# Regrouping the matmuls of an attention kernel's prelude by kind, and a second buffer for the staged value products

## The chip, the core and the metric

The kernel runs on one core of one Trainium2 chip, all in fp32. The metric is device time in microseconds of one execution; the time shown is the median of several executions. Lower is better.

## What is computed

One gated cross-attention block with a feed-forward layer behind it, for x of shape (4, 2048, 512) and a context of shape (4, 77, 384), with 16 heads of 64:

```
n   = layernorm(x)
sim = (n @ Wq)_h @ (ctx @ Wk)_h^T * 64**-0.5          # per head h, 77 keys
att = softmax(sim) @ (ctx @ Wv)_h                     # heads joined again
x   = x + tanh(g_xattn) * (att @ Wo + bo)
x   = x + tanh(g_ffn) * (layernorm(x) @ W[k] + b[k])  # k = argmax(log_softmax(logits) + gumbel(u)), of 8
```

## The kernel before

The kernel folds weights together once, in a prelude, and then works on 16 groups of 512 tokens. For every head it needs two products that don't depend on the tokens. M is the head's query weight, with its row means taken out, times the head's keys (512 features by 80 padded keys by 4 batches). VO is the head's values times its slice of Wo (320 padded key rows by 512 features). With these a group needs three large products: scores = x M, attention output = p VO, feed-forward = y W. Each is done by `Seven`, a Strassen-Winograd scheme: seven products of half-size blocks instead of eight, with sums of the operand blocks made beforehand. For the operands that stay, `weight_sum(w, n)` makes them: blocks 0 to 3 of `m` hold M, `weight_sum(m, 0)` fills block 5, `(m, 1)` changes block 3, `(m, 2)` fills block 4 and `(m, 3)` fills block 6. For the moving ones, `xc[i].sum("T1")` to `sum("T4")` make them in `tq`. `product(s)` issues the matmuls of step s and `post(s)` takes a finished partial sum out of PSUM into `snap`, or adds it there. Steps 0, 2, 4 and 6 of a `Seven` go on adding to the same PSUM bank, so step 2 must wait until `post(0)` has copied what step 0 left.

The order on every engine is written by hand: the statements run in program order, and each engine keeps that order. Seven PSUM banks are handed out in turn. The SP queue issues nearly all DMAs, in order.

The prelude before the change, with the lines of the profile:

- `project_k(p)` (L266, evicted by ScalarE at L271) and `centre_wq(p)` (L283 to L291) for the eight pairs p of heads.
- `build_m(q, ...)` makes two of the four 128-feature quarters of M. One `m_head` is one matmul with 64 rows of contraction (L296), and two copies out of PSUM (L302 into `m` for batch 0, L303 into a staging area for batches 1 to 3). Quarters with even number are copied by ScalarE, odd ones by VectorE. The two heads of a pair lie in the two halves of the array's rows and are issued alternately.
- `project_v(p)` makes the values of one pair: three matmuls with 128 rows (L266) and one copy (L276) by ScalarE and VectorE in turn. Before the change each of the eight calls stands behind one pair's four `m_head` in `build_m`.
- The staging areas of M are `stages[0]` (blocks 4 to 6 of `m`), `stages[1]` and `stages[2]` (the two halves of `vo`) and `stages[3]` (`m_st`, in the buffer that later holds the scores `s`). At the end of each half of M four DMAs (L315, 960 KB each) store two areas to DRAM.
- `build_vo(p, engines)` makes VO of one pair: six matmuls with 64 rows (L331, the last two with 64 columns), six copies with a scale (L334 on VectorE, L336 on ScalarE), and four DMAs to DRAM (L340, 512 KB, and L341, 128 KB). The staging for the copies is `vo_st`, five areas in `vo`.
- `gates0` to `gates2` compute the two tanh and the choice k in small VectorE and ScalarE instructions; `gather()` (L246, L248) fetches row block k of W and of b by indirect DMA from the GpSimd queue. `sum_wf` (L631 to L633, GpSimd) and `mean_wf` (L639, a matmul with a tile of ones, and the copy L640) take the column means of W.
- Then come group 0's scores in three `Seven`: s0 for two of the five chunk pairs, s1 for two, s2 for one. Before the change pair 0 of VO stands ahead of s0, and pairs 1 and 2 stand behind steps 2 and 5 of s0. `x_columns` (L407) and `s_rows` (L515) are 32 by 32 transposes on VectorE. Pairs 3 to 7 of VO are made between group 1's scores, before and after the change.

Of the kernel before, what the change touches and what calls it, by code (L numbers as in the profile page):

```python
# [14 lines left out]
P = 128  # L15
# [4 lines left out]
def flamingo_block_kernel(  # L20
# [33 lines left out]
    nc = tc.nc  # L54
    NT, D = x.shape
# [7 lines left out]
    NP = H // 2  # L63
# [4 lines left out]
    KH = NK // 2  # L68
# [5 lines left out]
    T2 = T // 2  # L74
    NG = T // 32
# [12 lines left out]
    def bank(name):  # L88
        return pm.tile([P, 512], F32, tag="mm", name=name)

    m_d = dp.tile([B - 1, P, 4, 2, KH * P], F32, name="m_d")
    vo_d = dp.tile([H, BP, D], F32, name="vo_d")
# [3 lines left out]
    BLK = {(0, 0): 0, (0, 1): 1, (1, 1): 2, (1, 0): 3}  # L96
    m = cp.tile([P, 7, 2, KH, P], F32, tag="m")
# [7 lines left out]
    snap = cp.tile([P, NCC * ID], F32, tag="snap")  # L105
# [8 lines left out]
    def flat(t):  # L114
        n = len(t.shape) - 1
        names = " ".join("abcdef"[:n])
        return t.rearrange(f"p {names} -> p ({names})")

    def weight_sum(w, n, engine=None):

        to, a, b_, op = ((5, 0, 3, ALU.subtract), (3, 3, 2, ALU.add), (4, 3, 0, ALU.subtract),
                         (6, 1, 4, ALU.subtract))[n]
        (engine or nc.gpsimd).tensor_tensor(flat(w[:, to]), flat(w[:, a]), flat(w[:, b_]), op)

    m_f, vo_f, wf_f = flat(m), flat(vo), flat(wf)
# [6 lines left out]
    def row_tile(name):  # L132
        return wp.tile([P, NG, P], F32, tag="row", name=name, bufs=3)
# [9 lines left out]
    t = wp.tile([P, NK * T + KH * T2], F32, tag="pT", name="wq")  # L143
# [3 lines left out]
    xg, ys, ts_ = {}, {}, {}  # L147
# [41 lines left out]
    def by_chunk(t):  # L189

        return t.rearrange("p (a q e) -> p q a e", a=NA, e=32)

    def chunked(t):
        return t.rearrange("p (q a e) -> p q a e", a=NA, e=32)
# [21 lines left out]
    def gates0():  # L216
        nc.scalar.activation(tg, gg, AF.Tanh)
        nc.vector.tensor_reduce(st[:, 0:1], lg, AX.X, ALU.max)
        nc.vector.tensor_scalar(z, lg, st[:, 0:1], None, ALU.subtract)
        nc.scalar.activation(ez, z, AF.Exp)  # L220

    def gates1():
        nc.vector.tensor_reduce(st[:, 1:2], ez, AX.X, ALU.add)
        nc.scalar.activation(st[:, 2:3], st[:, 1:2], AF.Ln)
        nc.scalar.activation(l2, uu, AF.Ln)
        nc.scalar.activation(l2, l2, AF.Ln, scale=-1.0)

    def gates2():
        nc.vector.tensor_scalar(z, z, st[:, 2:3], None, ALU.subtract)
        nc.vector.tensor_tensor(z, z, l2, ALU.subtract)  # L230
        nc.vector.tensor_reduce(st[:, 3:4], z, AX.X, ALU.max)

        nc.vector.tensor_scalar(ez, z, st[:, 3:4], None, ALU.is_equal)
        nc.vector.tensor_tensor(ez, ez, rev, ALU.mult)
        nc.vector.tensor_reduce(st[:, 4:5], ez, AX.X, ALU.max)
        nc.vector.tensor_scalar(st[:, 5:6], st[:, 4:5], -1.0, float(OPS), ALU.mult, ALU.add)
        nc.vector.tensor_scalar(st[:, 6:7], st[:, 5:6], float(D), None, ALU.mult)
        nc.vector.tensor_scalar(st[:, 7:8], st[:, 5:6], float(NA), None, ALU.mult)
        nc.vector.tensor_scalar(rows[:, :NDC], rows[:, :NDC], st[:, 6:7], None, ALU.add)
        nc.vector.tensor_scalar(rows[:, NDC:], rows[:, NDC:], st[:, 7:8], None, ALU.add)  # L240
        nc.vector.tensor_copy(rows_u, rows)
    def gather():
        t = row_tile("wfr").rearrange("p g j -> p (g j)").rearrange("p (c d) -> p c d", c=NDC)
        for c in range(NDC):
            at = bass.IndirectOffsetOnAxis(ap=rows_u[:, c : c + 1], axis=0)
            nc.gpsimd.indirect_dma_start(out=t[:, c, :], out_offset=None, in_=W, in_offset=at)  # L246
        at = bass.IndirectOffsetOnAxis(ap=rows_u[:, NDC:], axis=0)
        nc.gpsimd.indirect_dma_start(out=bf_r, out_offset=None,  # L248
                                     in_=b.rearrange("o (a j) -> (o a) j", j=P), in_offset=at)
        nc.gpsimd.tensor_scalar(bo_c, bo_c, tgx, None, ALU.mult)  # L250
        nc.gpsimd.tensor_scalar(bf_r, bf_r, tgf, None, ALU.mult)
        return t
# [20 lines left out]
    def project_v(p):  # L273
        d = vT[p].rearrange("p r b k -> p b k r")
        copy = nc.vector.tensor_copy if p % 2 else nc.scalar.copy
        copy(d, project(wv, p, cT).rearrange("p (b k r) -> p b k r", b=B, r=R))  # L276
# [25 lines left out]
        copy(to_m[:, :, q % 2, :, ts(h, R)], src[:, 0].rearrange("p (o k) r -> p o k r", o=2))  # L302
        copy(to_d, src[:, 1:])  # L303

    def build_m(q, p0, p1, stages, v0=None):

        for p in range(p0, p1):
            for dq, dh in ((0, 0), (1, 1), (1, 0), (0, 1)):
                m_head(q + dq, 2 * p + dh, stages[dq])
            if v0 is not None:  # L310
                project_v(v0 + p - p0)
        if p1 == NP:
            for dq in range(2):
                for o in range(2):
                    nc.sync.dma_start(  # L315
                        out=m_d[:, :, BLK[o, (q + dq) // 2], (q + dq) % 2].rearrange("b p k -> p b k"),
                        in_=stages[dq][:, :, ts(o, KH * P)])


    vo_st = []  # L320

    def build_vo(p, engines):
        n = 0
        for c in range(3):
            r = min(P, BP - c * P)
            for hh in range(2):
                stg = vo_st[(2 * p + hh) % len(vo_st)]
                hr = ts(hh, DH)
                v = vT[p][hr].rearrange("p r b k -> p (r b k)")
                ps = bank("ps_vo")  # L330
                nc.tensor.matmul(ps[:r, :], v[:, ds(c * P, r)], wo[hr, p, :], start=True, stop=True)  # L331
                src, dst = by_chunk(ps[:r, :]), chunked(stg[:r, c, :])
                if engines[n % len(engines)] == "D":
                    nc.vector.tensor_scalar(dst, src, tgx[:r], None, ALU.mult)  # L334
                else:
                    nc.scalar.activation(dst, src, AF.Copy, scale=tgx[:r])  # L336
                n += 1
        for hh in range(2):
            d, stg = vo_d[2 * p + hh], vo_st[(2 * p + hh) % len(vo_st)]
            nc.sync.dma_start(out=d[0 : 2 * P].rearrange("(c r) e -> r c e", r=P), in_=stg[:, 0:2])  # L340
            nc.sync.dma_start(out=d[2 * P :], in_=stg[: BP - 2 * P, 2])  # L341

# [151 lines left out]
    norms, xc, yc, sc, pT = ({} for _ in range(5))  # L494

    def x_columns(i):
        t = column_tile("xc")
        tqs = {f"T{n + 1}": tq[:, n] for n in range(4)}
        xc[i] = Columns(t, **tqs)
        for q in range(NDC):  # L500
            to_columns(t, xg[i], q)
# [90 lines left out]
    def store(f, g0=0, n=NG, queues=(nc.sync,)):  # L592
        for a in range(NA):
# [4 lines left out]
    stages = [t[:, : (B - 1) * NK * P].rearrange("p (b k) -> p b k", b=B - 1) for t in  # L598
              (m_f[:, 4 * 2 * KH * P :], vo_f, vo_f[:, NP * D :], s_f)]
# [9 lines left out]
    for a in range(NA):  # L609
        nc.gpsimd.dma_start(out=bo_c[ts(a, 32)], in_=bo[ts(a, P)].rearrange("(q e) -> e q", e=32))  # L610
    nc.sync.dma_start(out=wo, in_=Wo.rearrange("(c p) f -> p c f", p=P))
    build_m(0, 0, NP // 2, stages[:2])
    build_m(0, NP // 2, NP, stages[:2], 0)
    x_columns(0)
    for t in ("T1", "T2", "T3", "T4"):
        xc[0].sum(t)
    weight_sum(m, 0)
    build_m(2, 0, 2, stages[2:], NP // 2)
    gates0()
    build_m(2, 2, NP // 2, stages[2:], NP // 2 + 2)  # L620
    gates1()
    build_m(2, NP // 2, NP, stages[2:])
    for n in range(1, 4):
        weight_sum(m, n, nc.gpsimd if n == 3 else nc.vector)
    for u_ in (vo_f[:, : NP * D], vo_f[:, NP * D :]):
        for e in range(u_.shape[1] // (3 * D)):
            vo_st.append(u_[:, ts(e, 3 * D)].rearrange("p (c e) -> p c e", c=3))

    def sum_wf(wfr):
        t = wf_f[:, :D]  # L630
        nc.gpsimd.tensor_tensor(t, wfr[:, 0, :], wfr[:, 1, :], ALU.add)  # L631
        nc.gpsimd.tensor_tensor(t, t, wfr[:, 2, :], ALU.add)
        nc.gpsimd.tensor_tensor(t, t, wfr[:, 3, :], ALU.add)  # L633

    wf_mean = wf_f[:, ds(5 * D, D)]

# [29 lines left out]

    n = norms[0]
    norms[1] = n1 = Norms(1)
    build_vo(0, "AD")
    s0 = scores0(0)  # L670
    for s in range(6):
        s0.product(s)
        if s == 0:
            gates2()
            wfr = gather()
        if s in (2, 5):
            build_vo(1 + s // 3, "AD")
        if s == 3:
            n.stats(xg[0], 0, 0, NG)
        s0.post(s)  # L680
    x_columns(1)
    for k in range(2):
# [106 lines left out]
    for i in range(1, NGRP):  # L789
        j, f, nx = i - 1, i - 2, i + 1  # L790
        n = norms[i]
# [126 lines left out]
        for s in range(6):  # L918
# [16 lines left out]
            if 2 <= s:  # L935
                k = (0, 2, 3, 5, 6)
# [6 lines left out]
    n = norms[NGRP] = Norms(NGRP)  # L943
# [145 lines left out]
```

## Time and profile before

| | before |
|---|---|
| median of 3 runs | 1253.28 us (1252.87 to 1254.22) |
| the profiled execution's own time | 1252.23 us |
| its span, first to last instruction | 1250.3 us |
| TensorE matmul busy | 1237.8 us, 99% |
| VectorE, ScalarE, GpSimd busy | 911.6, 683.0, 888.9 us |
| granted TensorE clock | 0.997 |

The profile is of one execution. Its page gives the busy time of each engine, the span in 40 slices, the DMA queues, the chain of waits that ended last, and groups of instructions by source line. "PE" is TensorE, "DVE" VectorE, "ACT" ScalarE, "POOL" GpSimd. A matmul of fp32 stands as two instructions in the trace. Two matmuls in different row halves of the array overlap, so their durations may not be added up; the distance from one start to the next may.

### The profile page before, as it was taken

What the parts mean: (1) busy time and instruction counts of PE and PEld (TensorE: products, weight loads), DVE (VectorE), ACT (ScalarE), POOL (GpSimd) and SP (SyncE); (2) the same over time, 40 slices, a digit from 0 to 9 for tenths busy, and PEclk for the clock granted to TensorE, in tenths of its full rate; (3) what the DMA queues carried; (4) which work ended last, traced back from release to release, by engine and by line L of the source; (5) the groups of instructions that cost most, each with busy time, mean ns of one, the idle gap of its engine ahead of it and who ended that gap; (6) DMA issues with size and microseconds to landing.
All of it is one profiled execution on the core that took longest, in us unless ns stands there. A gap on an engine that the chain in (4) does not pass through costs nothing.

```text
span 1250.3 us, 16985 instructions
## 1 busy us (share of the span) xinstructions
PE 1237.8 (99%) x5704; PEld 1059.4 (85%) x5704; DVE 911.6 (73%) x1855; ACT 683.0 (55%) x1957; POOL 888.9 (71%) x482
## 2 busy tenths in 40 slices
PE   9999999999999999999999999999999999999996
PEld 6575888888888888888888888888888888888885
DVE  5789876667976766787776767776776877766577
ACT  3539554738274573827456382745638274564823
POOL 4348885867967786685968778575977877575766
PEclk9999999999999999999999999999999999999998
DMA  9777300314014030303106030212305120010102
GB/s 261 296 210 237 92 1 1 68 42 110 1 34 118 1 68 1 68 23 106 26 1 152 1 68 2 48 20 85 68 1 112 41 57 12 1 34 1 34 2 67
DMA packets 95221, 80.27 MB, mean 64 GB/s; under 512 B 3856, under 2 KB 83088, under 8 KB 95136
## 3 DMA queue, kind: packets, MB, share of 16 engines
q1 hardware_dynamic: 92768, 76.74, 24.1%
q10 hardware_dynamic: 1760, 1.34, 0.4%
q0 software_dynamic: 608, 1.13, 0.3%
q8 instruction: 45, 0.74, 0.3%
q14 instruction: 40, 0.33, 0.1%
HBM read 44.07 MB, written 35.13 MB: 63 GB/s over the span
## 4 chain that ended last, share of the span: by engine, by line
PE 94%; DVE 3%; ACT 1%; POOL 1%; issue 0%; DVEq 0%; ACTq 0%; POOLq 0%
PE ps_s L461 37%; PE ps_a L461 36%; PE ps_f L461 15%; PE ps_kv L266 2%; PE ps_vo L331 2%; PE ps_m L296 2%; ACT s L532 1%; POOL s L543 1%; DVE s L515 1%; DVE pT L552 0%; PE ps_w L167 0%; DVE snap L486 0%; DVE t L412 0%; DVE vo L334 0%; DVE sm L539 0%
## 5 line engine op out<-in xcount | busy, mean ns | idle before, releaser
L461 PE MATMUL ps_a<-pT,vo 128*128 128x256 f32 x2240 | 486.2, 379 | 0.0
L461 PEld LDWEIGHTS ps_a<-pT,vo 128*128 128x128 f32 x2240 | 425.6, 190 | 57.9
L532 ACT ACTIVATE s<-s,nmx,up 128x77 f32<-128x77 f32 x1024 | 355.6, 446 | 0.8 <-DVE nmx L526 0.8
L432 POOL TENSOR_TENSOR pT<-pT 128x1280 f32<-128x1280 f32 x64 | 185.8, 2904 | 171.9 <-PE ps_a L461 162.3
L461 PE MATMUL ps_s<-tq,m 128*128 128x256 f32 x1280 | 290.8, 380 | 0.3 <-ACT snap L467 0.3
L461 PEld LDWEIGHTS ps_s<-tq,m 128*128 128x128 f32 x1280 | 242.5, 190 | 36.7 <-issue 1.6
L467 ACT COPY snap<-ps_s 128x512 f32<-128x512 f32 (+1 forms) x188 | 93.5, 514 | 287.6 <-DVE t L412 131.4
L461 PE MATMUL ps_s<-xc,m 128*128 128x256 f32 x960 | 221.4, 380 | 0.0
L461 PEld LDWEIGHTS ps_s<-xc,m 128*128 128x128 f32 x960 | 182.0, 190 | 29.0 <-DVE vo L334 2.4
L543 POOL TENSOR_TENSOR s<-s,sm 128x1232 f32<-128x1232 f32 x64 | 145.2, 2270 | 48.2 <-DVE sm L540 48.1
L486 DVE TENSOR_TENSOR snap<-snap,ps_s 128x512 f32<-128x512 f32 (+1 forms) x141 | 83.5, 593 | 122.0 <-PE ps_s L461 117.9
L461 PE MATMUL ps_f<-tq,wf 128*128 128x256 f32 x512 | 118.5, 379 | 0.5 <-DVE snap L486 0.4
L552 DVE STREAM_TRANSPOSE pT<-s 128x512 f32<-128x512 f32 x160 | 101.0, 677 | 16.8 <-POOL s L543 16.8
L432 POOL TENSOR_TENSOR tq<-xc,tq 128x512 f32<-128x512 f32 x64 | 85.3, 1332 | 34.8 <-PE ps_f L461 32.3
L393 POOL TENSOR_TENSOR r<-r,neghalf 32x16 f32<-32x16 f32 (+1 forms) x33 | 93.1, 2831 | 23.1 <-DVE r L388 22.6
L461 PEld LDWEIGHTS ps_f<-tq,wf 128*128 128x128 f32 x512 | 97.1, 190 | 14.4 <-issue 0.7
L539 DVE TENSOR_REDUCE sm<-s 128x16 f32<-128x1232 f32 x64 | 91.5, 1429 | 20.7 <-ACT s L532 20.6
L515 DVE STREAM_TRANSPOSE s<-snap 128x512 f32<-128x512 f32 x156 | 99.8, 684 | 6.1 <-ACT snap L467 3.9
L524 DVE TENSOR_REDUCE ps_st<-s 128x16 f32<-128x1232 f32 x64 | 92.4, 1444 | 2.1
L432 POOL TENSOR_TENSOR tq<-xc 128x512 f32<-128x512 f32 x64 | 81.5, 1273 | 13.6 <-DVE xc L407 12.3
L461 PE MATMUL ps_f<-xc,wf 128*128 128x256 f32 x384 | 90.7, 379 | 0.0
L467 ACT COPY snap<-ps_f 128x512 f32<-128x512 f32 x63 | 36.9, 585 | 88.9 <-PE ps_f L461 85.9
(127 smaller groups left out, 1186.0 us busy)
## 6 DMA issues: line engine op xcount, KB each, us to landing
xg<-in_x_dram SPq DMA_DIRECT2D x64, 256.0 KB, 5.6
out_dram<-y SPq DMA_DIRECT2D x60, 256.0 KB, 4.2
vo<-vo_d SPq DMA_DIRECT2D x16, 640.0 KB, 5.6
vo_d<-vo SPq DMA_DIRECT2D x16, 512.0 KB, 3.5
m<-m_d SPq DMA_DIRECT2D x12, 640.0 KB, 4.0
m_d<-vo SPq DMA_DIRECT2D x4, 960.0 KB, 6.1
wq<-in_WqT_dram SPq DMA_DIRECT2D x8, 256.0 KB, 7.0
wq<-in_Wo_dram SPq DMA_DIRECT2D x1, 2048.0 KB
```

The lines of the kernel that those rows point to most:

```text
L266: nc.tensor.matmul(ps[:, :n], w[:, c, ts(p, P)], keys[:, c].rearrange("p b j -> p (b j)"), start=(c == 0), stop=(c == NCC - 1))
L393: nc.gpsimd.tensor_tensor(r, r, neghalf[:32, : r.shape[1]], ALU.pow)
L432: (engine or nc.gpsimd).tensor_tensor(self.at[name], self.at[a], self.at[b_], op)
L461: nc.tensor.matmul(self.ps[r][:, n, :], self.w(blk, c, pair), self.cols(cname, c), start=(first and n == 0 and c == 0), stop=(c == h - 1), ...
L467: nc.scalar.copy(dst, self.ps[r])
L486: nc.vector.tensor_tensor(c, c, self.ps[r], ALU.add)
L515: nc.vector.transpose(key_chunk(sc[i], k), cols.rearrange("p (g h r) -> p g h r", h=HA, r=R))
L524: nc.vector.tensor_reduce(mx, head(i, h), AX.X, ALU.max)
L532: nc.scalar.activation(head(i, h)[:, g, :], head(i, h)[:, g, :], AF.Exp, scale=norms[i].up[:, g : g + 1], bias=nmx[h][:, g : g + 1])
L539: nc.vector.tensor_reduce(sm, head(i, h), AX.X, ALU.add)
L543: nc.gpsimd.tensor_tensor(head(i, h), head(i, h), sums[h].unsqueeze(2).to_broadcast([P, NG, J]), ALU.mult)
L552: nc.vector.transpose(pT[i].all[:, k, :].rearrange("p (g h r) -> p g h r", h=HA, r=R), key_chunk(sc[i], k))
```

## The change

M is built in two runs of 32 heads with nothing between the heads, and the values of all eight pairs are made between the two runs. The smaller work of the prelude (x_columns of group 0 and its sums, the gates, the statistics of group 0) stands between the values now. Three pairs of VO follow the second run in a row, and then group 0's scores with no VO inside s0. Pair 0 of VO is staged in `snap`, which is free of the value weights by then; later pairs use the five areas in `vo`. Quarter 3 of M is stored behind pair 0's VO. `weight_sum(m, 1)` and `(m, 2)` move from VectorE to GpSimd, and `gather()` stands behind the weight sums.

```diff
-    def build_m(q, p0, p1, stages, v0=None):
-        for p in range(p0, p1):
+    def build_m(q, stages):
+        for p in range(NP):
             for dq, dh in ((0, 0), (1, 1), (1, 0), (0, 1)):
                 m_head(q + dq, 2 * p + dh, stages[dq])
-            if v0 is not None:
-                project_v(v0 + p - p0)
-        if p1 == NP:
-            for dq in range(2):
-                for o in range(2):
-                    nc.sync.dma_start(
-                        out=m_d[:, :, BLK[o, (q + dq) // 2], (q + dq) % 2].rearrange("b p k -> p b k"),
-                        in_=stages[dq][:, :, ts(o, KH * P)])
+    def store_m(q, stage):
+        for o in range(2):
+            nc.sync.dma_start(out=m_d[:, :, BLK[o, q // 2], q % 2].rearrange("b p k -> p b k"),
+                              in_=stage[:, :, ts(o, KH * P)])
+    def stage_of(h):
+        return vo_st[h if h < 2 else 2 + (h - 2) % (len(vo_st) - 2)]
...
-    build_m(0, 0, NP // 2, stages[:2])
-    build_m(0, NP // 2, NP, stages[:2], 0)
-    x_columns(0)
-    for t in ("T1", "T2", "T3", "T4"):
-        xc[0].sum(t)
-    weight_sum(m, 0)
-    build_m(2, 0, 2, stages[2:], NP // 2)
-    gates0()
-    build_m(2, 2, NP // 2, stages[2:], NP // 2 + 2)
-    gates1()
-    build_m(2, NP // 2, NP, stages[2:])
-    for n in range(1, 4):
-        weight_sum(m, n, nc.gpsimd if n == 3 else nc.vector)
-    for u_ in (vo_f[:, : NP * D], vo_f[:, NP * D :]):
+    for u_ in (snap, vo_f[:, : NP * D], vo_f[:, NP * D :]):
...
+    build_m(0, stages[:2])
+    for q in range(2):
+        store_m(q, stages[q])
+    for p in range(NP):
+        project_v(p)
+        if p == 0:
+            x_columns(0)
+            for t in ("T1", "T2", "T3", "T4"):
+                xc[0].sum(t)
+            weight_sum(m, 0)
+        if p == 2:
+            gates0()
+        if p == 3:
+            gates1()
+        if p == 4:
+            norms[0].stats(xg[0], 0, 0, NG)
+        if p == 6:
+            gates2()
+    build_m(2, stages[2:])
+    store_m(2, stages[2])
+    for n in range(1, 4):
+        weight_sum(m, n)
+    wfr = gather()
+    build_vo(0, "AD")
+    store_m(3, stages[3])
+    for p in range(1, 3):
+        build_vo(p, "AD")
...
-    build_vo(0, "AD")
     s0 = scores0(0)
     for s in range(6):
         s0.product(s)
-        if s == 0:
-            gates2()
-            wfr = gather()
-        if s in (2, 5):
-            build_vo(1 + s // 3, "AD")
-        if s == 3:
-            n.stats(xg[0], 0, 0, NG)
         s0.post(s)
```

More of the change, by code (lines that the diff above doesn't have):

```diff
@@ L326, in build_vo @@
             for hh in range(2):
-                stg = vo_st[(2 * p + hh) % len(vo_st)]
+                stg = stage_of(2 * p + hh)
                 hr = ts(hh, DH)
@@ L338, in build_vo @@
         for hh in range(2):
-            d, stg = vo_d[2 * p + hh], vo_st[(2 * p + hh) % len(vo_st)]
+            d, stg = vo_d[2 * p + hh], stage_of(2 * p + hh)
             nc.sync.dma_start(out=d[0 : 2 * P].rearrange("(c r) e -> r c e", r=P), in_=stg[:, 0:2])
```

## The prediction

> **What bounds the kernel now.** I read the page first (busy times and the chain of waits), then the chain in order of time for the first 80 us, then the timelines of VectorE, GpSimd and the SP queue beside it.
>
> ```profile
> PE 1237.8 (99%) x5704; PEld 1059.4 (85%) x5704; DVE 911.6 (73%) x1855; ACT 683.0 (55%) x1957; POOL 888.9 (71%) x482
> PE 94%; DVE 3%; ACT 1%; POOL 1%; issue 0%; DVEq 0%; ACTq 0%; POOLq 0%
> ```
>
> TensorE is the bound, end to end. Its only waits after the start are 0.35 us ahead of one score matmul and 0.4 us in the last part. So whatever TensorE saves in the prelude comes off the end, if nothing else becomes late. The chain in order of time (start, length, what) shows how long each kind of matmul takes in each neighbourhood:
>
> ```profile
> 5.98 12.44 PE ps_kv L266 x48
> 18.42 5.60 PE ps_m L296 x40
> 24.02 1.81 PE ps_kv L266 x6
> 25.84 1.28 PE ps_m L296 x8
> ...
> 47.47 4.51 PE ps_m L296 x32
> 51.97 2.72 PE ps_vo L331 x12
> 54.70 5.38 PE ps_s L461 x24
> 60.07 2.95 PE ps_vo L331 x12
> 63.02 5.38 PE ps_s L461 x24
> 68.40 2.97 PE ps_vo L331 x12
> 71.37 0.03 issue
> 71.40 0.07 DVE vo L334
> ...
> 72.73 2.40 DVE xc L407 x4
> 75.13 1.20 DVE s L515 x2
> ...
> 76.41 0.59 ACT snap L467
> 77.05 5.45 PE ps_s L461 x24
> ```
>
> The reader is to compare like with like. Eight M instructions take 1.12 us inside a run (5.60 / 5) and 1.28 us between values. Six value instructions take 1.81 us; by the key run (12.44 / 48, times 320 / 308 columns) they should take 1.62. A VO pair takes 2.72 us behind M, which also uses 64 rows, and 2.95 behind scores.
>
> **The change part by part.** Time zero for each part is T, the end of the last M matmul (51.97 before).
>
> *M and values.* One value group between M groups costs (1.81 - 1.62) + (1.28 - 1.12) = 0.35 us, so 0.18 per change between 64-row and 128-row matmuls. After the change: 128 M instructions at 0.1405 = 17.98, 48 value instructions at 0.2693 = 12.93, two changes 0.35; 31.26 instead of the 33.55 from 18.42 to 51.97. Saved 2.3 us; T becomes 49.7.
>
> *VO and scores.* Before, from T to the restart at 77.05, 25.08 us. After: three VO pairs at 2.72 = 8.16, nine score steps of eight matmul instructions at 0.216 (9.50 us for 44 later on) = 15.54, one change 0.2; 23.9. Saved 1.2 us, of which 0.35 is the stall. That stall is s1's `post(0)` behind VectorE's last VO copy, x_columns and s_rows. Without the VO copy (0.74) the row of VectorE work is 0.67 + 2.4 + 1.2, ScalarE adds 0.6, and TensorE has three steps, 5.2 us, to do meanwhile; nothing is left over, nothing is gained beyond. A VO pair behind a VO pair isn't in the trace: between 2.56 (no change of mode) and 2.95, and I take 2.72, the row that follows another 64-row kind; that is -0.3 to +0.5 us for two pairs.
>
> *Copies out of PSUM.* The M runs are longer now, with VectorE and ScalarE taking every other head:
>
> ```profile
> 19.41 0.23 DVE L302 COPY m<-ps_m 128x80 f32<-128x80 f32 x1
> 19.56 0.40 DVE L303 COPY vo<-ps_m 128x240 f32<-128x240 f32 x1
> 19.87 0.23 DVE L302 COPY m<-ps_m 128x80 f32<-128x80 f32 x1
> ```
>
> From head to head VectorE needs 0.46 us when it is behind (19.41 to 19.87), ScalarE 0.36 to 0.39, and TensorE delivers one per engine each 0.56. The Trainium skill speaks against the change here: "TensorEngine Tiling (Array Packing)", Performance Considerations, says that tiling speeds up TensorE but not the copies out of PSUM, which can become the bound. With the durations as they stand (0.24 + 0.40 = 0.64 a head) that would be so: 16 heads take 10.2 us against 9.0, and with the lag that VectorE brings to the second run the seven banks (1.7 us of matmuls ahead) would be short by about 0.9 us. The starts decide, since neighbouring copies overlap: 0 us, up to 0.9 in the range.
>
> *What moves onto VectorE between the values:* x_columns 2.5, gates0 and gates1 0.6, the statistics 3.2, gates2 2.2, four value copies of 0.78. From 28.0 (end of M's copies) and held to the values' own times this ends at 41.9, TensorE starts the second run at 40.6. The lag of 1.3 us fits into the banks (head 6 needs the last value's bank at 42.3). If gates2's first instruction is held up as before (1.17 us beside GpSimd's weight sum, against 0.2 for its like), M waits 0.6 us. x_columns needs group 0's tokens: their four loads were issued by 18.0 and take 9 us, before 28.
>
> *Weight sums on GpSimd.* Three of 2.9 us from T + 0.6 to T + 9.4. Step 1 of s0 uses the first at T + 10.1, step 2 the second at T + 11.8, step 5 the third at T + 17; hidden. VectorE loses 3.0 us of work, which nobody was waiting for.
>
> *DMAs and the SP queue.* M's first four stores are issued at 28 rather than 33.9, but wait in the queue behind Wo, whose bytes are followed by M's without a gap before the change too; they still end near 46, and the sum into block 5 still starts near 42.5. After T the order is two M stores, four of pair 0, two M stores, then pairs 1 and 2. New waits: s0's `post(0)` (ScalarE, with all later posts behind it, and TensorE's step 2 waiting) needs the first store of pair 0 out of `snap`. M's stores began to move at 53.5 and ran 960 KB in 2.5 us, the first landing 0.6 us after its last byte. So two M stores end at T + 6.5, 512 KB more at T + 7.9, landed at T + 8.5; `post(0)` wants it at T + 10.1. Hidden with 1.6 us left for ScalarE, 2.5 in all before a matmul is late. [...]The later posts need pair 0's other stores, 0.8 MB more, at T + 11.8: 2 us of bytes, so T + 10.5, hidden too. Pair 2 goes where quarter 2 of M was staged; landing T + 7.1, wanted T + 6.3 to 7.2; its banks are wanted at T + 10. The last M store holds the buffer of the scores: its bytes end near T + 16, s_rows wants it at T + 22.
>
> *The gather* is issued at T + 9.4 as before (61.44), now behind weight sums instead of behind gates2. TensorE reaches the ones-matmul at T + 29.1 instead of 30.4 (82.33).
>
> ```profile
> 75.47 0.60 POOL L251 TENSOR_SCALAR bf_r<-bf_r,tg 128x128 f32<-128x128 f32 x1 [7.57 <-DMA bf_r<-in_b_dram,rows_u]
> 78.73 1.27 POOL L633 TENSOR_TENSOR wf<-wf,wfr 128x512 f32<-128x512 f32 x1
> ```
>
> GpSimd waited for the gather until T + 23.5 and had the sum at T + 28.0. So 1.1 us of slack is left of 2.3: zero cost if the gather lands as before, and all that it is later by beyond 1.1 otherwise.
>
> Sum: 2.3 + 1.2 = 3.5 us off the profiled 1252.23, that is 1248.7 (span 1246.8). The median of the runs stands 1.05 us above the profiled execution: 1249.8.
>
> **The rivals.**
>
> *Gather a little late.* The DMA queue holds 4.6 MB of stores when the gather starts, against some 2.5 before. For it: the four row fetches already took 9.9 us each. Against it: with stores pending before, they moved 1 MB in about 6 us beside them. Two to three us later costs 1 to 2: 1250.8 to 1251.8, within 0.2% of before. Chance 0.14.
>
> *Smaller savings*: VectorE's lag reaches the banks (0.6 to 0.9), or VO pairs in a row cost 2.95 each (0.5): 1250.4 to 1251.2. Chance 0.12.
>
> *The gather comes last (slower).* If its packets move only after the stores and group 2's token loads, which follow in the same queue: 5.9 MB from T + 6.5 at 390 KB/us, and the loads, in 512-byte pieces, at half of that, end near T + 27; then the gather 2.7, GpSimd 4.6: the sum at T + 35, TensorE idle for 5.9 us at the ones-matmul: 1255.7. It decides from where b's row lands after T + 28.1 (before: T + 23.5). Against it: the fair share seen before. Chance 0.10; another 0.04 for a wait on pair 0's store of the same size.
>
> *Nothing changes* because TensorE isn't freed: the excess of 0.18 per change stands in every neighbourhood, so I give that no share of its own.
>
> **How the numbers follow.** The likeliest case, 0.60, is 3.5 us saved, 1248.8 to 1250.6. A measurement of this kernel can tell about 0.2% (2.5 us) from no change, so faster means below 1250.8. With the edge of the second rival: faster 0.62, within 0.2% 0.24, slower 0.14. The range reaches from the likeliest case with cheap VO pairs (1248.8) over the two mild rivals to the runs' own spread: 1252.8.
>
> **What would show it.** Right: the chain has one M run of 9.0 us from 18.4, values of 13 us, M again, T at 49.7; VO 8.1 us; scores undivided to a step at T + 23.9 with no idle time; ScalarE's first copy into `snap` waiting for TensorE, not for a DMA. Wrong: idle TensorE at the ones-matmul behind GpSimd; M instructions above 0.15 us in the second run behind VectorE; "snap" waiting on the VO store.

## The result, and the profile after

| | before | after |
|---|---|---|
| median of 7 runs each | 1253.50 us (1252.36 to 1254.22) | 1249.18 us (1248.72 to 1249.89) |
| the profiled execution: span, own time | 1250.3, 1252.23 us | 1247.1, 1249.17 us |

The ratio is 0.9967, with a 95% interval of 0.9958 to 0.9977: the changed kernel is faster by 0.33%. Line numbers after are those of before plus one from `build_vo` on (VO L332, scores L462, VectorE's posts L487), and the ones-matmul is L655.

First the page of the changed kernel (busy times, and the shares of the chain of waits), then its chain in order of time: start, length, what.

```profile
PE 1234.9 (99%) x5704; PEld 1061.0 (85%) x5704; DVE 908.8 (73%) x1853; ACT 683.6 (55%) x1957; POOL 894.8 (72%) x484
PE 94%; DVE 2%; ACT 1%; DMA 1%; POOL 0%; issue 0%; SPq 0%; DVEq 0%; ACTq 0%; POOLq 0%
```

```profile
6.45 12.44 PE ps_kv L266 x48
18.89 8.81 PE ps_m L296 x64
27.71 13.12 PE ps_kv L266 x48
40.83 8.81 PE ps_m L296 x64
49.64 8.57 PE ps_vo L332 x36
58.21 21.04 PE ps_s L462 x96
79.25 0.86 PE ps_w L655 x2
```

TensorE runs the prelude in five unbroken pieces (keys, M, values, M, VO), then the scores. The same number of matmuls takes 2.9 us less busy time than before (1234.9 instead of 1237.8). From 18.89 to 49.64 M and the values take 30.75 us instead of 33.55. Its waits, over the whole span (what waited, for what, total us, times, longest):

```profile
PE ps_w L167 <- DVE tq L163: 1.5, 1, 1.5
PE ps_f L462 <- DVE snap L487: 0.4, 1, 0.4
```

The stall of 0.35 us ahead of s1 is gone, and no new one has come. The timelines of ScalarE (first line) and GpSimd show why; the bracket is the idle time before an instruction and what ended it:

```profile
60.21 0.58 ACT L468 COPY snap<-ps_s 128x512 f32<-128x512 f32 x1 [1.29 <-PE ps_s L462]
50.08 8.83 POOL L123 TENSOR_TENSOR m<-m 128x1280 f32<-128x1280 f32 x3 [5.47 <-ACT m L302]
72.74 0.60 POOL L251 TENSOR_SCALAR bf_r<-bf_r,tg 128x128 f32<-128x128 f32 x1 [7.20 <-DMA bf_r<-in_b_dram,rows_u]
76.00 1.27 POOL L621 TENSOR_TENSOR wf<-wf,wfr 128x512 f32<-128x512 f32 x1
```

`post(0)` waited for TensorE, not for the store of pair 0. The three weight sums end at 58.9. GpSimd had the gathered row of b at 72.7 and the sum of W's rows at 77.3; TensorE came for it at 79.3, so about 2.0 us were to spare.

**A ruler for all runs.** The profiles show that the prelude's first matmul of M starts anywhere from 18.1 to 19.4 us, with the warm-up ahead of it, whatever the kernel. So spans are compared in three stretches between starts of TensorE instructions: A from the first M matmul to the first of VO, B from there to the ones-matmul, C from there to the first feed-forward matmul with an operand out of `tq`. After that point every kernel of the study takes 1079.4 to 1079.8 us more. Each row of A, B and C is one profiled execution (us).

| kernel | A | B | C | A+B+C | median of its runs | ratio to before, 95% |
|---|---|---|---|---|---|---|
| before | 33.46 | 30.52 | 88.56 | 152.54 | 1253.9 beside the experiments | |
| after | 30.65 | 29.62 | 88.56 | 148.83 | 1249.18 | 0.9967 [0.9958, 0.9977] |
| after_again | 30.65 | 29.62 | 88.55 | 148.82 | 1249.69 | 0.9962 [0.9949, 0.9976] |
| m_only | 30.80 | 35.39 | 88.68 | 154.87 | 1254.38 | 1.0005 [0.9996, 1.0013] |
| m_alone | 30.65 | 33.74 | 88.56 | 152.95 | 1254.21 | 1.0002 [0.9993, 1.0011] |
| m_old_staging | 30.65 | 30.52 | 88.57 | 149.74 | 1249.76 | 0.9967 [0.9955, 0.9979] |
| values_in_twos | 33.60 | 29.62 | 88.57 | 151.79 | 1251.38 | 0.9981 [0.9974, 0.9988] |
| vo_only | 34.47 | 33.69 | 88.68 | 156.84 | 1256.59 | 1.0024 [1.0017, 1.0030] |
| vo_alone | 34.46 | 31.49 | 89.29 | 155.24 | 1255.82 | 1.0020 [1.0011, 1.0030] |
| vo_gather_first | 38.32 | 31.51 | 88.57 | 158.40 | 1258.55 | 1.0037 [1.0023, 1.0051] |
| m_stores_first | 30.65 | 33.33 | 88.56 | 152.54 | 1252.83 | 0.9995 [0.9986, 1.0004] |
| gather_late | 30.65 | 33.26 | 89.29 | 153.20 | 1252.91 | 0.9998 [0.9989, 1.0007] |
| vo_full_width | 30.65 | 28.77 | 89.27 | 148.69 | 1249.28 | 0.9965 [0.9951, 0.9978] |
| three_full_width | 30.65 | 28.77 | 88.58 | 148.00 | 1248.45 | 0.9955 [0.9942, 0.9969] |

The change saves 2.81 in A and 0.90 in B, and keeps all of it in C.

### The profile page after: what moved, and what is told of

It is laid out like the page before. It is cut to its first block, busy times and chain, and to the rows that moved or that the text cites. A ratio compares the mean times of both kernels' runs of the same rounds, so it can differ in the third digit from the quotient of the medians.

```text
span 1247.1 us, 16992 instructions
## 1 busy us (share of the span) xinstructions
PE 1234.9 (99%) x5704; PEld 1061.0 (85%) x5704; DVE 908.8 (73%) x1853; ACT 683.6 (55%) x1957; POOL 894.8 (72%) x484
## 4 chain that ended last, share of the span: by engine, by line
PE 94%; DVE 2%; ACT 1%; DMA 1%; POOL 0%; issue 0%; SPq 0%; DVEq 0%; ACTq 0%; POOLq 0%
PE ps_s L462 37%; PE ps_a L462 36%; PE ps_f L462 15%; PE ps_kv L266 2%; PE ps_vo L332 2%; PE ps_m L296 1%; ACT s L533 1%; DVE s L516 0%; DMA vo<-vo_d 0%; DVE pT L553 0%; PE ps_w L167 0%; DVE t L413 0%; DMA vo_d<-vo 0%; DVE snap L487 0%; POOL xc L559 0%
## 5 line engine op out<-in xcount | busy, mean ns | idle before, releaser
L462 PE MATMUL ps_a<-pT,vo 128*128 128x256 f32 x2240 | 486.2, 379 | 0.0
L462 PEld LDWEIGHTS ps_a<-pT,vo 128*128 128x128 f32 x2240 | 425.6, 190 | 57.9
L462 PE MATMUL ps_s<-tq,m 128*128 128x256 f32 x1280 | 290.6, 380 | 0.0
L462 PEld LDWEIGHTS ps_s<-tq,m 128*128 128x128 f32 x1280 | 242.6, 190 | 36.2 <-issue 1.6
L462 PE MATMUL ps_s<-xc,m 128*128 128x256 f32 x960 | 221.0, 379 | 0.0
L462 PEld LDWEIGHTS ps_s<-xc,m 128*128 128x128 f32 x960 | 182.2, 190 | 27.5 <-DVE vo L335 1.6
L487 DVE TENSOR_TENSOR snap<-snap,ps_s 128x512 f32<-128x512 f32 (+1 forms) x141 | 83.7, 593 | 130.4 <-PE ps_s L462 126.3
L462 PE MATMUL ps_f<-tq,wf 128*128 128x256 f32 x512 | 118.5, 379 | 0.5 <-DVE snap L487 0.4
L462 PEld LDWEIGHTS ps_f<-tq,wf 128*128 128x128 f32 x512 | 97.1, 190 | 14.4 <-issue 0.7
L462 PE MATMUL ps_f<-xc,wf 128*128 128x256 f32 x384 | 90.7, 379 | 0.0
```

The costliest lines, as they stand in the source:

```text
L462: nc.tensor.matmul(self.ps[r][:, n, :], self.w(blk, c, pair), self.cols(cname, c), start=(first and n == 0 and c == 0), stop=(c == h - 1), ...
L487: nc.vector.tensor_tensor(c, c, self.ps[r], ALU.add)
```

## The experiments

**M's two runs by themselves: m_only, m_alone, m_old_staging.** m_only is the changed kernel with pairs 1 and 2 of VO back inside s0:

```diff
-    for p in range(1, 3):
-        build_vo(p, "AD")
...
         s0.product(s)
+        if s in (2, 5):
+            build_vo(1 + s // 3, "AD")
```

> The changed kernel with pairs 1 and 2 of VO put back behind steps 2 and 5 of group 0's first score product; the two M runs and the values between them stay. Theory (each change of TensorE between 64-row and 128-row matmuls costs about 0.18 us): the stretch from the first M matmul to the last takes 30.7 us as in the changed kernel instead of 33.55, so about 2.8 us of the gain stay and 0.9 to 1.3 us are lost: 1250.0 to 1250.8. Rival (the gain comes from group 0's scores, where the stall of 0.35 us and VectorE's late copies were): most of the gain is lost, 1252 or more.

A fell to 30.80 as the theory has it, and the whole gain was lost again in B, which is 35.39 instead of the changed kernel's 29.62. The trace gave the wait to GpSimd's weight sums:

```profile
PE ps_s L462 <- POOL m L123: 3.0, 1, 3.0
```

So the first theory was that the sums are hidden only behind three VO pairs. m_alone tests it by putting two of the sums back on VectorE:

```diff
     for n in range(1, 4):
-        weight_sum(m, n)
+        weight_sum(m, n, nc.gpsimd if n == 3 else nc.vector)
```

> The kernel before with the M part alone (M in two runs with all values between them, its norms, gates and stores as in the change), VO pairs where they were, and the sums of slices 1 and 2 on VectorE as before, so that the first scores do not wait for GpSimd as in m_only. Theory (the two parts add, and m_only lost its gain only by that wait): M and values take 30.8 us instead of 33.55, no wait of TensorE for GpSimd ahead of step 1 of s0, the stall of 0.35 us ahead of s1 stays; median about 2.6 us under the kernel before (ratio 0.998). Rival (VectorE's two sums of 1.49 us, standing between the last M copies and pair 0's copies, now come when TensorE is 2.8 us earlier and hold it): 1 to 2 us of the gain lost, ratio 0.9988 to 0.9993.

That theory fell: the wait was again 3.0 us long. The trace of m_alone shows the real releaser (timelines of GpSimd, ScalarE and TensorE, one line each):

```profile
53.81 2.89 POOL L123 TENSOR_TENSOR m<-m 128x1280 f32<-128x1280 f32 x1 [8.96 <-DVE m L123]
58.85 0.58 ACT L468 COPY snap<-ps_s 128x512 f32<-128x512 f32 x1 [5.25 <-DMA vo_d<-snap]
59.53 1.97 PE L462 MATMUL ps_s<-tq,m 128*128 128x256 f32 x8 [3.00 <-issue]
```

The last sum ended at 56.7, 2.8 us before TensorE went on. `post(0)` is the one that ended when TensorE restarted (58.85 and 0.58). It had waited for pair 0's store to land, because pair 0 is staged in `snap` and `post(0)` writes `snap`. In m_only the last sum ended at 58.65 and `post(0)` at 58.62, so that trace by itself cannot tell them apart, and the sum took the blame. m_old_staging therefore is m_alone with pair 0 put back where it was staged before:

```diff
-    for u_ in (snap, vo_f[:, : NP * D], vo_f[:, NP * D :]):
+    for u_ in (vo_f[:, : NP * D], vo_f[:, NP * D :]):
...
-        return vo_st[h if h < 2 else 2 + (h - 2) % (len(vo_st) - 2)]
+        return vo_st[h % len(vo_st)]
```

> m_alone with pair 0 staged in VO's own buffer as in the kernel before, not in the snapshot's place. Theory (what held m_only and m_alone was not the weight sums: TensorE stood 3.0 us for step 2 of s0 in both, until post(0) had copied step 0's bank into the snapshot, and post(0) waited for pair 0's stores to land at T+8.7; the sums had ended at 56.71 in m_alone, 2.8 us before the restart): no such wait, M and values 30.8 us instead of 33.55, from the first product of M to the first of ps_f 149.7 us (152.47 before), ratio 0.9978. Rival (the weight sums or the gather hold it after all): the wait of about 3 us stays, 152.9 us from M to ps_f, ratio 1.000.

A is that of the changed kernel and B that of the kernel before, both to 0.01 us. ScalarE's `post(0)` now waits for TensorE:

```profile
54.94 0.59 ACT L468 COPY snap<-ps_s 128x512 f32<-128x512 f32 x1 [1.25 <-PE ps_s L462]
```

By the trace, M's part alone is worth 2.8 of the change's 3.7 us. By the medians it cannot be told from the whole change. The staging in `snap` brings a wait of 3.0 us with one pair ahead of s0; in the changed kernel the three pairs in a row cover it.

**Fewer values between the M groups: values_in_twos.** Two pairs of values stand between M groups of 16 heads (the last two groups have 8), in place of all eight between two runs: eight changes of kind instead of two.

```diff
-    build_m(0, stages[:2])
+    build_m(0, stages[:2], 0, 4)
+    values(0)
+    values(1)
+    build_m(0, stages[:2], 4, 8)
...
```

> The changed kernel with the values in four groups of two pairs inside the M runs: eight changes of row mode instead of two, nothing else. Theory: six changes at 0.16 to 0.18 us, so the stretch of M and values takes 1.0 us more than in the changed kernel (31.7 us), 1250.2. Rival (VectorE and ScalarE, relieved by longer runs, made the difference, not the changes): no difference or a difference that shows as idle TensorE before an M matmul.

B is the changed kernel's, A is 2.95 longer. The pieces of TensorE's timeline:

```profile
23.14 3.50 PE L266 MATMUL ps_kv<-cT,snap 128*128 128x320 f32 x12
29.27 3.15 PE L296 MATMUL ps_m<-wf,wqp 64*128 64x320 f32 x18 [0.28 <-DVE wq L276]
35.78 4.58 PE L296 MATMUL ps_m<-wf,wqp 64*128 64x320 f32 x32
```

By start to start, twelve value instructions take 3.43 us (23.14 to 26.57) and 32 M instructions 4.51 where nothing holds them (35.78 to 40.28). Together with the chains of both kernels (6, 12 and 48 values in 1.81, 3.43 and 13.12; 8, 32 and 64 M instructions in 1.28, 4.51 and 8.81) all undisturbed runs fit one rule: a run of n values takes 0.269 n + 0.20, a run of n M instructions 0.134 n + 0.22. So a change between the two kinds costs about 0.2, and the six added here about 1.3.

The rest, 1.7, isn't price of changes. By the starts it stands in two M runs alone, of 32 instructions each: the first took 4.99 us and the second 5.78 (26.57 to 32.35), in place of 4.51. The second is the edit's: VectorE came to x_columns more than 4 us earlier (23.7 instead of 28.4), waited 2.3 us there for the tokens of group 0, and TensorE ran short of banks behind it (the 0.28 in the bracket is a part). The first is of this execution: M began as early as 18.15, VectorE was still busy with centring the query weights, and took M's first copy 1.51 us behind M's start instead of 0.88 (in m_only 1.19, with 0.16 lost in the same place). These parts are not the same in every run: eight of the 17 have spans of 1248.3 to 1249.1, less than the earliest M start seen (18.08) with this sum and 1079.42 behind it would make, 1249.3.

**VO in a row without M's runs: vo_only, vo_alone, vo_gather_first.** vo_only is the kernel before with three pairs in a row ahead of s0, pair 0 in `snap`, and the sums on GpSimd:

```diff
-    build_vo(0, "AD")
+    for p in range(3):
+        build_vo(p, "AD")
     s0 = scores0(0)
...
-        if s in (2, 5):
-            build_vo(1 + s // 3, "AD")
```

> The kernel before with the other part alone: pair 0 of VO staged in snap, pairs 0 to 2 in a row ahead of group 0's scores, the three weight sums on GpSimd; values stay between the M groups. Theory: 0.9 to 1.3 us faster than before (1252.2 to 1252.6), the stretch of M and values unchanged at 33.5 us, no idle TensorE at the scores. Rival (the gain is in the scores): 3 us or more faster.

It came out slower than before. The row of VO itself took 8.67 us from start to start, as in the changed kernel. But M's stores of both late quarters stood ahead of pair 0's, so `post(0)` waited for pair 0's store and TensorE for `post(0)`, 2.2 us, with a lower clock behind the wait (last section). In A, all three kernels of this group carry 1.0 us of a VectorE instruction held up by GpSimd (last section too). vo_alone puts one of these quarters behind pair 0, as the change does, and two sums back on VectorE:

```diff
-        weight_sum(m, n)
+        weight_sum(m, n, nc.gpsimd if n == 3 else nc.vector)
...
         build_vo(p, "AD")
+        if p == 0:
+            for o in range(2):
+                nc.sync.dma_start(out=m_d[:, :, BLK[o, 1], 1].rearrange("b p k -> p b k"),
+                                  in_=stages[3][:, :, ts(o, KH * P)])
```

> The kernel before with three VO pairs in a row and pair 0 staged in the snapshot's place, the sums of slices 1 and 2 on VectorE as before, and the stores of M's slice 3 placed behind pair 0's stores (in vo_only all four of M's stores stood ahead of them). Theory: VO and the scores of group 0 save what they saved in the change, 0.9 us, if post(0) no longer waits for pair 0's store; ratio 0.9993. Rival (M's slices 0 to 2 are still stored late, at the end of M, so pair 0's store still lands after T+10 and post(0) waits, with the lower clock behind the wait): the same 1 to 3 us slower as vo_only, ratio 1.001 to 1.002.

The store was no longer waited for; other things were. Its gather, on GpSimd's timeline:

```profile
65.84 1.07 POOL L246 DMA_INDIRECT wfr<-in_W_dram,rows_u  x1 [6.58 <-PE ps_s L464]
```

That is 13.3 us after VO's first matmul instead of 9.6, because gates2, which names the row, stood behind nine VO copies on VectorE. TensorE waited 0.4 us for W's sum at the ones-matmul and once more, 0.24, behind it, and VectorE's sums ahead of its first VO copy made the row of VO 0.7 longer. vo_gather_first takes these away: sums on GpSimd, and the statistics, gates2 and the gather ahead of the row:

```diff
     gates1()
+    norms[0].stats(xg[0], 0, 0, NG)
+    gates2()
...
+    wfr = gather()
...
-            gates2()
-            wfr = gather()
```

> The kernel before with all of the change except M's two runs: three VO pairs in a row, pair 0 in the snapshot's place, slice 3's stores behind pair 0's, sums on GpSimd, and gates2, the norms' sums and the gather ahead of the VO row (in vo_alone gates2 stood behind the row, its VectorE instructions waited for the nine VO copies and the first gather was issued at T+13.1). Theory: the 0.9 us of VO and scores that the change saves, ratio 0.9993, from M to ps_f 151.5 us (155.17 in vo_alone). Rival (gates1 and gates2 now meet the weight sum of slice 0 on GpSimd in the middle of M, where M's copies stand behind them): some 0.7 to 1.5 us of stall in M, ratio 1.000 to 1.0005.

The rival, that M's copies stand behind the gates, was right in this and too small in size: 4.6 us above before by the medians. But no weight sum was in the way of gates2, as the rival had it; GpSimd's next sum began at 59.0. TensorE's waits:

```profile
PE ps_m L296 <- DVE m_st L303: 2.4, 1, 2.4
PE ps_m L296 <- ACT vo L303: 0.7, 1, 0.7
```

In the middle of M, 3.2 us of statistics and 2.5 of gates2 hold up VectorE's copies and TensorE has no free bank. B is 31.51 instead of the changed kernel's 29.62 without any wait in it: the row of VO, begun at the low clock behind that stop, took 10.55 us instead of 8.67. In the changed kernel the same VectorE instructions stand between values, where VectorE has time. So the row of VO wants the gates done early, and of the places tried only the one between the values cost nothing. No run here got a gain out of VO's row without M's runs.

**Stores of M ahead of pair 0's: m_stores_first.**

```diff
+    store_m(3, stages[3])
     build_vo(0, "AD")
-    store_m(3, stages[3])
```

> The changed kernel with the stores of M's slice 3 ahead of pair 0's stores. Theory: pair 0's first stores land about 5 us later, at T+13.6 instead of T+8.6, post(0) waits for them (it wants them at T+10.1), and TensorE stands at step 2 of s0 for 1.5 to 3 us: 1251 to 1253, more if the granted clock drops. Rival (the store of slice 3 is not ready before pair 0's anyway, or its bytes do not stand in the way): no wait, 1249.2.

The theory held, by the median inside its range, by the ruler a little above:

```profile
PE ps_s L462 <- ACT snap L468: 3.2, 2, 2.4
63.12 0.59 ACT L468 COPY snap<-ps_s 128x512 f32<-128x512 f32 x1 [4.64 <-DMA vo_d<-snap]
```

B is 3.71 longer, and by the starts of TensorE's instructions all of it lies at the two stops, 2.7 and 1.0 us; the table's 3.2 counts each from the end that the profile gives the matmul before, later than the next one could have started. By the ruler, this one line in the SP queue is worth as much as the change.

**A late gather: gather_late.**

```diff
     for n in range(1, 4):
         weight_sum(m, n)
+    for _ in range(2):
+        weight_sum(m, 3)
     wfr = gather()
```

> The changed kernel with two more weight sums of 2.9 us on GpSimd ahead of the gather (slice 3's sum repeated, its result written again). Theory (the profile of the changed kernel shows 2.0 us between the end of the sum of gathered rows and the ones-matmul): TensorE waits 3.8 us at the ones-matmul, and all of it stays to the end: 1253.0, or up to 1254.6 if the granted clock drops behind the wait as it did in m_only. Rival (other work fills it, or the gather comes earlier because fewer transfers are in its way later): under 2 us, 1250 to 1251.

```profile
PE ps_w L657 <- POOL wf L621: 3.5, 1, 3.5
```

The two sums of 2.9 us made W's sum 5.4 us later, counted from VO's first matmul (33.2 instead of 27.8). By the starts the slack had been 1.8 us; the other 3.6 stand in B, and 0.7 more in C. So the slack read from the profile was real, and by this profile nothing fills what lies beyond it. The median is 3.2 above after_again and 0.9 below the profiled execution, so in other runs it was less.

**The last 64 columns: vo_full_width, three_full_width.** VO's last product has 64 columns of weights where the others have 128. vo_full_width makes it 128 wide (64 of them are then computed a second time and not used):

```diff
-            r = min(P, BP - c * P)
+            lo = P - min(P, BP - c * P)
...
-                nc.tensor.matmul(ps[:r, :], v[:, ds(c * P, r)], wo[hr, p, :], start=True, stop=True)
-                src, dst = by_chunk(ps[:r, :]), chunked(stg[:r, c, :])
+                nc.tensor.matmul(ps, v[:, ds(c * P - lo, P)], wo[hr, p, :], start=True, stop=True)
+                src, dst = by_chunk(ps[lo:, :]), chunked(stg[lo:, c, :])
```

> The changed kernel with the third block of every VO product taken 128 columns wide, over the last 128 of the 320 key rows, of which the last 64 are copied out and stored as before; TensorE then never goes from 128 to 64 columns. Theory (a change of columns costs like a change of rows): three VO pairs in a row take about 7.8 us instead of 8.57, and each of the five pairs between group 1's scores 0.15 less: 1.5 us faster than the changed kernel, 1247.7. Rival (the excess over 2.56 us a pair is something else, such as the wait of the weight loads): no difference, 1249.2. A copy that starts at row 64 could be slower; then ScalarE or VectorE would be late and show as idle TensorE.

B fell by 0.85, and C gave 0.71 of it back. In pairs 3 to 7 the copies of rows 64 to 127 are slower (two of ScalarE's take 1.40 us instead of 1.26, four of VectorE's 2.85 instead of 2.72), and ScalarE is full from 94 to about 122 us with the exponentials. That these copies are what costs the 0.71 is the likely reading; what the next run shows is that the loss comes with the wide products of pairs 3 to 7. New waits of TensorE:

```profile
PE ps_s L462 <- DVE sn L487: 0.3, 1, 0.3
PE ps_f L462 <- POOL tq L433: 0.3, 1, 0.3
```

three_full_width does it for pairs 0 to 2 alone:

```diff
+            lo, w = (P - r, P) if p < 3 else (0, r)
```

> The changed kernel with the last 64 rows of VO computed as part of a full 128-column product, in pairs 0 to 2 alone; pairs 3 to 7 as in the change, so their copies do not get slower. Theory (in vo_full_width the 0.85 us gained in the prelude was given back because the copies of pairs 3 to 7 were slower on ScalarE, which bounds that part): VO row 7.8 us, ones-matmul 0.85 earlier and the end too; 1248.4, 0.85 under the changed kernel. Rival (what bounds from 93 us on starts from something the prelude's TensorE does not set, a transfer or VectorE's chain): the end stays, 1249.2.

Its chain of waits:

```profile
49.68 7.72 PE ps_vo L333 x36
57.41 21.05 PE ps_s L463 x96
78.45 0.86 PE ps_w L656 x2
```

B keeps its 0.85 and C is that of the changed kernel: 1248.45 us. This is the best version of the study by the profile, 0.8 us under the changed kernel; its five runs (1247.96 to 1248.98) and after_again's five (1248.44 to 1249.75) overlap.

**The mark: after_again.** The changed kernel, unaltered:

> The changed kernel once more, unaltered, as the mark for the three beside it. 1249.2; the spread of its start (the first product of the values) shows what part of a span is run to run.

A, B and C are the same to 0.01 us as in the first profile, while M starts 0.52 later and the span is 0.5 longer. So these two executions differ by the warm-up ahead of the prelude.

## Why the prediction came out

It gave 1249.8 us; 1249.18 was measured. The parts held in kind. That the sum came so near was luck in part: 0.5 us too little for M and the values and 0.3 too much for VO and the scores went opposite ways. The sizes of its terms:

- *M and values*: 2.3 predicted, 2.8 measured (chain). The term that was too small is the price of a change of rows: 0.18 was taken, and by the rule of values_in_twos it is about 0.21; 14 changes fewer at that price are 2.9, close to the 2.8 measured. The 0.14 for an M instruction "inside a run" came from the run of 40 that carries a change of its own; without it an instruction takes 0.134. The same reading gave 0.1405 for the long runs, which took 0.1377.
- *VO*: 8.16 predicted for three pairs, 8.57 measured, 2.86 a pair. The error is the choice of 2.72, the row behind M, for pairs behind pairs. Each pair ends with 64-column products, and the five changes of width in three pairs cost 0.85 us (vo_full_width). The starts of the changed kernel show where: 0.42 us from one 128-wide product to the next, 0.52 at every change of width, and 0.47 (to 64 columns) or 0.53 (back to 128) at the product behind it; that adds up to 0.84.
- *Scores*: the 96 instructions up to the ones-matmul took 21.04 us; at the 9.50 for 44 that was used, with 0.2 for the change, 20.9. So stretch B saved 0.9 and not 1.2, chiefly because of VO.
- *The stall ahead of s1*: gone, as said, and nothing was gained beyond it.
- *Copies out of PSUM*: the reading by starts, against the rule it was weighed with, held. VectorE's last value copy ended at 41.84 with M's second run begun at 40.83, and TensorE did not wait.
- *Pair 0's store*: wanted later than it lands, as said; by m_alone it lands 8.7 us after the last M matmul (58.85 less 50.15), predicted 8.5. m_stores_first shows the failure at the place that was named, step 2 of s0, at 3.7 us in all; the prediction had put it at the gather's 5.9.
- *The gather*: 1.1 us of slack was expected, 2.0 was there. W's sum came at T + 27.6 rather than T + 28.0, and TensorE came 0.5 later than predicted. The slower rival was of the right kind (gather_late), but its transfers did not come last.
- *Weight sums on GpSimd*: hidden; they end at 58.9 and TensorE shows no wait for them. What moving them off VectorE brings by itself was not tried with the three pairs in a row.

The sum, 3.5 us, against 3.7 on the ruler; the profiled execution shows 3.2 in its span (3.1 in its own time) because its M began 0.47 later. The medians differ by 4.3. The gap between that and 3.7 is not settled by a run. What speaks for a cause is the section on the hardware below: a hold that costs stretch A 1.0 us stood in all three other profiles of kernels with M's old order (one M run of 8 instructions takes 2.31 us there instead of 1.28), and not in the one profile of before. Some runs of before have spans of 1252.5, with M's start never seen beyond 19.44: 1252.5 - 19.44 - 1079.42 leaves 153.64 for A + B + C, 1.1 more than its profile shows. That these runs had the hold is inferred; they were not profiled.

What the prediction did not see is how the parts lean on each other. It added up savings. By the experiments, M's runs leave room for the gates between the values, early gates keep the row of VO from making the gather late (vo_alone, vo_gather_first), the row covers the store out of `snap` (m_alone), and the order of stores lets that store land in time (m_stores_first).

## What to carry to other kernels

Where matmuls of different shape alternate, read the price of a change from runs of different length of the same instruction (time = a n + c, n the number of instructions) and not from one long run, which carries a change too. When parts of a change are tried alone, ask first which of its buffers only another part makes free: here one staging buffer turned a gain of 2.8 us into nothing. And a releaser named in a table of waits is a candidate; the one to trust is that whose end and the waiter's start lie together in two kernels.

## What the runs showed of the hardware

**A small VectorE instruction held for a whole GpSimd instruction.** From VectorE's and GpSimd's timelines, first in vo_alone and then in before:

```profile
41.88 2.97 DVE L219 TENSOR_SCALAR z<-lg,st 128x8 f32<-128x8 f32 x1
41.94 2.88 POOL L123 TENSOR_TENSOR m<-m 128x1280 f32<-128x1280 f32 x1
```

```profile
42.16 0.23 DVE L219 TENSOR_SCALAR z<-lg,st 128x8 f32<-128x8 f32 x1
42.52 2.90 POOL L123 TENSOR_TENSOR m<-m 128x1280 f32<-128x1280 f32 x1 [0.25 <-DMA m_d<-m]
```

The same instruction on 8 values takes 0.23 us or 2.97. In vo_alone it came 0.1 us before the end of one GpSimd sum and lost to the next, the long sum of `m`, which followed without a gap (so in vo_only and vo_gather_first, 2.98 each); in before GpSimd happened to wait 0.25 us for a store, and it slipped through. Behind it stand M's copies, so A is 34.46 instead of 33.46. A gap is not what it takes, though. In the changed kernel the same instruction came 0.4 us before the end of a shorter GpSimd sum (of `tq`, at 32.43), waited for that and was done at 32.46, although another sum of `tq` followed as closely:

```profile
32.01 0.45 DVE L219 TENSOR_SCALAR z<-lg,st 128x8 f32<-128x8 f32 x1
32.40 1.26 POOL L433 TENSOR_TENSOR tq<-xc 128x512 f32<-128x512 f32 x1
```

The Trainium skill, "SBUF — State Buffer", section "SBUF: two separate sides", has the rule: certain VectorE instructions and GpSimd share a pair of ports as an exclusive lock, and the later one is blocked for the whole instruction. The rows of vo_alone agree. What decides which of two goes next when both stand ready is not settled here: in the eight other profiles with M in two unbroken runs it took 0.29 to 0.46 us. VectorE's copies out of PSUM ran on beside the same GpSimd sums (0.23 and 0.40 us each, as without one).

**The clock behind a wait.** After TensorE's wait of 3.0 us in m_only, the stretch from 60 to 65 us was granted 0.70 of the clock (the number after the POOL column), and eight score instructions took 2.94 us instead of 1.97:

```profile
60.00:65.00 5.00, 5.00 (x17) 2.04 (x15) 1.39 (x2) 1.95 (x3) 3.87 (x5) 0.70 1.01 348
```

In vo_only (2.2 us of waiting) it was 0.82, in vo_gather_first (2.4) 0.76. While it is low, score instructions start 0.43 us apart instead of 0.22. In m_alone, m_stores_first and gather_late (3.0, 2.4 and 3.5 us) the clock stayed at 1.00. The Trainium skill, "TensorE: Matmul & The Clock Gate", section "What's actually happening", puts the drop behind at least one idle window of about 3.4 us; here shorter waits were enough in three profiles of six, and the one wait longer than that had no drop behind it. So a wait is to be priced at its length or at up to 1.9 us more: m_only less m_alone is 1.65 in B and 0.12 in C, the eight score instructions behind vo_only's wait took 1.6 longer, and the row of VO in vo_gather_first 1.9. What decides between the two was not tried.
